# Graph convolution on one core: segment sums in one PSUM bank, edge attributes turned on chip, and VectorE's column picks moved to the end of each run

## The chip, the cores and the metric

The kernel runs on one core of a Trainium2 chip. The metric is the device time of one execution in microseconds (us): 3691.56 us is the median of 10 runs of the kernel before (3687.99 to 3696.28). Engines are named as in the profile: PE is TensorE (matrix products), DVE is VectorE, ACT is ScalarE, POOL is GpSimd, SP is SyncE. SP and POOL do no arithmetic here worth speaking of; they issue DMAs.

## The reference, cut to what matters

12,500 nodes carry 128 numbers each (32 scalars and 32 vectors of 3). 412,500 edges are sorted by target node; each has a source node, 4 attributes and 8 radial numbers.

```
f        = x @ W1            (128 -> features used by edges, and a part kept by the node)
e        = f[src]            gather by source node, 412,500 rows of 128 numbers
w        = gelu(gelu(ea8 @ Wm1) @ Wm2) @ Wp      128 weights per edge
message  = products of w, e and the 4 attributes ea4
n        = segment_sum(message, dst)
y        = keep * f_self + mix * (n @ W2)
out      = layernorm(x + y)
```

## The kernel before

The edges are cut into 806 **runs** of 512 (4 quarters of 128 edges, one edge per partition), and 4 runs make a **chunk**, so there are 202 chunks. One loop (`for s in range(NCH * CH + CH)`) goes over the runs; `s` is the run, `c, k = divmod(s, 4)` its chunk and its place in it. The order in which each of PE, ACT, DVE and SP issues its work is the order of the calls in this loop: the schedule is written by hand, and each engine works its list strictly in that order. POOL has a list too, but only of gathers.

A first stage of some 150 us loads `x`, writes `x @ W1` as `table` to memory and keeps `x` transposed in `xT`. Then, for each run `s`:

- **Gathering the rows of `f`.** `gather(s + 19)` (line 194) issues up to four indirect DMAs on POOL, one per quarter, 19 runs ahead into a ring of 20 tiles `G`. Three other ways take quarters off POOL: every 14th run one quarter is fetched row by row by SP (`aid`, L184); and `COLS = {DVE: 5, ACT: 7}` says that DVE takes one quarter in 5 runs and ACT one in 7. They **pick** 128 columns of `xT`, one at a time, by a node number that stands in a register: `pick_nodes` (L154) loads the registers of this run's share from on-chip memory (a `TENSOR_LOAD`), `pick` copies (L165 on DVE, L167 on ACT). `picked_rows` (L173, L174) multiplies the finished quarter by `W1`.
- **Weights.** `radial` (L458, L460), `mlp1` (L467, L471), `mlp2` (L482, L487) for a chunk, `weights` (L499) for two runs, on PE and ACT.
- **Messages.** `messages(s)` (L538, L541) is three products on DVE: weights from PSUM times gathered rows, into `M` of 128 x 4 quarters x 2 halves x 128.
- **Selection.** `select(c + 1)` (L525, L529), at k = 3, makes for each edge a row `S` of 4 attributes x 8 places: the attribute where the edge's target is the j-th of its quarter's 8 nodes, zero elsewhere.
- **Segment sums.** `segments(s - 1)` (L550) multiplies `S` by `M` on PE: 4 products with 32 columns of weights and 256 columns of data into a PSUM tile of 128 x 256 with a single buffer; ACT copies it to `SG` (L553). Of its 256 columns, only the first 128 are used for attribute 0 and only the last 128 for attributes 1 to 3.
- **Placing.** `placing(s)` (L559) makes on DVE a 128 x 128 matrix of zeros and ones; `place(c - 1)` (L566, L567), at k = 1, multiplies with it, two products a run, so that sums stand in a window of 32 nodes. `add(c - 1)` (L572, L577), at k = 2, loads four window positions into registers and adds the four windows into the sums `A` on DVE, one after the other.
- **Norm.** 24 times, when the chunk's nodes are complete, `norm` (L594 to L625) finishes 512 nodes. Four clears of the next sums (L365) follow, one a run.

The list of VectorE for one run is therefore: messages (3 products), placing, register load, picks (24 or 28 copies), and then, by k, the additions (k = 2) or the norm and the selection (k = 3) or a clear. The list of SP holds, besides the aid rows, two loads per chunk, of `ea8` (128 x 16 x 8) and `ea4` (128 x 16 x 4; L449), the latter in pieces of 16 bytes.

Of the kernel before, what the change touches and what calls it, by code (L numbers as in the profile page):

```python
# [44 lines left out]
STEPS = 12  # L45
COLS = {DVE: 5, ACT: 7}
COL_Q = {DVE: Q - 2, ACT: Q - 3}
# [5 lines left out]
def gnn_kernel(ctx: ExitStack, tc: tile.TileContext, x, src, dst, ea4, ea8, w1_0, w1_1, wm1, wm2,  # L53
# [54 lines left out]
    for e, per in COLS.items():  # L108
        picked[e], (t, k) = [], COL_TURN[e]
        while True:  # L110
            at = t + per + 1
            at += (k - at) % CH
            if at + 2 >= NS - 1:
                break
            picked[e].append((t, at, at + 2))
            t += per
    pick_of = {(e, s): i for e, g in picked.items() for i, (_, _, s) in enumerate(g)}
# [7 lines left out]
    def aid_load():  # L125


        nc.sync.dma_start(aid_at, sub(src, AID_FROM * SB + (Q - 1) * P, [[AID * SB, len(aided)], [1, P]]))
        nc.vector.tensor_scalar(aid_at, aid_at, float(4 * P), None, op0=OP.mult)
        for e, g in picked.items():  # L130
            cycle = CH // math.gcd(CH, COLS[e])
            for h in range(0, len(g), P):
                part = g[h:h + P]
                rows = cst.tile([len(part), P], I32, name=f"pick{len(pick_rows)}")
                for i in range(min(cycle, len(part))):
                    n = len(part[i::cycle])
                    nc.sync.dma_start(rows[i::cycle], sub(src, part[i][2] * SB + COL_Q[e] * P,
                                                          [[cycle * COLS[e] * SB, n], [1, P]]))
# [6 lines left out]
    def pick_nodes(e, s):  # L145

        per = COLS[e]
        i, t = divmod(s - COL_TURN[e][0], per)
        if not 0 <= i < len(picked[e]):
            return  # L150
        if t == 0:
            GT[e, i] = wk.tile([P, P], F32, name=f"gt{list(picked).index(e)}", bufs=3)
        r0, r1 = (n * (P // 4) // per * 4 for n in (t, t + 1))
        _, r = nc.values_load_multi_w_load_instructions(  # L154
            pick_rows[e, i][:, r0:r1], engines=[e], min_val=x_at, max_val=x_at + 4 * (N - 1),
            skip_runtime_bounds_check_because="addresses of columns")
# [137 lines left out]
    def clear():  # L294
        nc.vector.memset(wpost, 0.0)
        nc.vector.memset(ones, 1.0)
        nc.vector.memset(odd, 0.0)

    def weight_loads():
# [89 lines left out]

    raws = {}  # L390

    def load_raws(b):
        raws[b] = [load_run_rows(dst, b, NO_NODE), load_run_rows(src, b, 0)]

    def load_indices(b):
# [4 lines left out]
        for kind, raw in zip((1, 0), raws.pop(b)):  # L400
            f = wk.tile([P, SB], F32, name="rawf")
            nc.vector.tensor_copy(f[:ns, :], raw[:ns, :])
            if kind:
                g = wk.tile([P, SB], F32, name="rawr", bufs=1)
                off = against_window(f, g, ns)
# [14 lines left out]

    def load_run_rows(a, b, fill):
        ns = min(P, NS - b * P)
        part = b * P + ns == NS and REM < SB
        fl = ns - 1 if part else ns
        raw = wk.tile([P, SB], I32, name="raw")
# [8 lines left out]
    e4, e8, eT, H1, H2, WP, S, M, PL, SG, ST = {}, {}, {}, {}, {}, {}, {}, {}, {}, {}, {}  # L434

    def load_edges(b):
        s0 = b * CH
        ns = min(CH, NS - s0)
        e4[b] = wk.tile([P, CH, Q, 4], F32, name="e4", bufs=EDGES_AHEAD)
# [3 lines left out]
        if part:  # L443
            nc.vector.memset(e4[b][:, fl], 0.0)
        if fl < CH:
            nc.vector.memset(e8[b][:, fl:], 0.0)
        for a, t, n in ((ea8, e8[b], RAD), (ea4, e4[b], 4)):
            if fl:
                nc.sync.dma_start(t[:, :fl].rearrange("p s q k -> p (s q) k"),  # L449
                                  sub(a, s0 * SB * n, [[n, P], [P * n, fl * Q], [1, n]]))  # L450
            if part and RQ:
                nc.sync.dma_start(t[:, fl, :RQ, :], sub(a, (s0 + fl) * SB * n, [[n, P], [P * n, RQ], [1, n]]))
            if part and RP:
                nc.sync.dma_start(t[:RP, fl, RQ, :], sub(a, ((s0 + fl) * SB + RQ * P) * n, [[n, RP], [1, n]]))

# [64 lines left out]
    def select(c):  # L520

        n = min(CH, NS - c * CH)
        b, r = divmod(c * CH, P)
# [3 lines left out]
                                .to_broadcast([P, n, Q, J]), op=OP.is_equal)  # L527
        S[c] = wk.tile([P, CH * Q, 4, J], F32, name="S")
        nc.vector.tensor_tensor(S[c][:, :n * Q],  # L529
                                oh[:, :n].rearrange("p s q j -> p (s q) j")[:, :, None, :]  # L530
                                .to_broadcast([P, n * Q, 4, J]),
                                e4[c][:, :n].rearrange("p s q k -> p (s q) k")[:, :, :, None]
                                .to_broadcast([P, n * Q, 4, J]), op=OP.mult)

# [10 lines left out]
    def segments(s):  # L545

        c, r = divmod(s, CH)
        pt = ps.tile([P, 2 * P], F32, name="seg", bufs=1)
        for q in range(Q):
            nc.tensor.matmul(pt[q * W:(q + 1) * W, :], S[c][:, r * Q + q].rearrange("p k j -> p (k j)"),  # L550
                             M[s][:, q].rearrange("p a u -> p (a u)"), start=True, stop=True)
        SG[s] = wk.tile([P, 2 * P], F32, name="sg", bufs=CH + 2)
        nc.scalar.activation(SG[s], pt, AF.Copy)  # L553

    def placing(s):

        b, r = divmod(s, P)
        PL[s] = wk.tile([P, P], F32, name="pl", bufs=CH + 1)
        nc.vector.tensor_scalar(PL[s], iota, colv[b][:, r:r + 1], None, op0=OP.is_equal)  # L559

    def place(c):
        ns = min(CH, NS - c * CH)
        ST[c] = pt = ps.tile([P, CH, 4, W], F32, name="m", bufs=1)
        for k in range(ns):
            s = c * CH + k
            nc.tensor.matmul(pt[:, k, 0, :], SG[s][:, :P], PL[s][:, :W], start=True, stop=True)  # L566
            nc.tensor.matmul(pt[:, k, 1:, :].rearrange("p a n -> p (a n)"), SG[s][:, P:], PL[s][:, W:],  # L567
                             start=True, stop=True)

# [187 lines left out]
    with tc.manual_schedule(engines={PE, ACT, DVE, SP}):  # L757
# [7 lines left out]
        for b in range(min(3, NG)):  # L765
# [3 lines left out]
        loads = list(weight_loads())  # L769
        extra = {2: lambda: load_edges(0), 4: lambda: load_raws(0), NG // 2: lambda: load_indices(0),  # L770
                 NG // 2 + 3: make_w1b, NG // 2 + 5: make_ws, NG - 6: lambda: radial(0), NG - 4: lambda: mlp1(0),
# [36 lines left out]
        for s in range(NCH * CH + CH):  # L808
# [7 lines left out]
            if s % P == P // 2 and (s // P + 1) * P < NS:  # L816
                load_indices(s // P + 1)
            for t in range(P // ROWS):
                a = s + AID_LEAD - t * STEPS // (P // ROWS)
                if a in aided:  # L820
                    aid(a, t)
# [9 lines left out]
            if k == (0 if end else 1) and 0 < c <= NCH:  # L831
                place(c - 1)
            for e in picked:
                if (e, s + 2) in pick_of:
# [57 lines left out]
```

## Time and profile before

| what | value |
|---|---|
| median of 10 runs | 3691.56 us (3687.99 to 3696.28) |
| the profiled execution, its own time | 3696.46 us |
| its span, first to last instruction | 3694.7 us |
| busy: PE, DVE, ACT, POOL | 2878.0, 3061.6, 2277.2, 2764.9 us |
| granted TensorE clock, mean | 0.783 |
| DMA moved, mean | 244.14 MB, 66 GB/s |

A page of the profile gives groups of instructions by line: engine, operation, tiles written and read, count; then busy us and mean ns of one; then the idle time of the engine ahead of them and what ended it. "issue" is idle time that ended without anything that the profile can name, for example while the engine's own sequencer was busy with instructions that are not counted as work (register loads, semaphore operations). Names with q (DVEq) are such instructions of a sequencer. The profile's span is 1.8 us below the execution's own time, and that is 4.9 us above the median of the runs.

### The profile page before, as it was taken

The page shows a single profiled execution, that of the slowest core. Times are in us where ns is not written, and L with a number is a line of the kernel's source. Part 1 is how long each engine was busy: PE and PEld are TensorE (multiplying, and loading weights), DVE is VectorE, ACT ScalarE, POOL GpSimd, SP SyncE. Part 2 cuts the span into 40 slices and gives each one's busy share as a digit, 9 for nine tenths or more (in the row PEclk, how much of TensorE's full clock was granted, in tenths as well). Part 3 has the DMA queues.
Part 4 walks back from the last instruction along what each step waited for, and adds up shares of the span by engine and source line. Part 5 has one row for each costly group of instructions (what it writes and reads, how often), then busy time and mean ns, then how long its engine had stood idle before and what let it go on. Part 6 is the DMA issues. An engine that isn't in the chain of part 4 may idle for free. (4 is left out here: it accounts for less than half of the span.)

```text
span 3694.7 us, 117877 instructions
## 1 busy us (share of the span) xinstructions
PE 2878.0 (78%) x24857; PEld 2046.5 (55%) x24857; DVE 3061.6 (83%) x25248; ACT 2277.2 (62%) x16665; POOL 2764.9 (75%) x2906
## 2 busy tenths in 40 slices
PE   5788788777788877778778788878787888777787
PEld 5555565455456555555555455555555655555555
DVE  3699898889898888887888888878888888788885
ACT  2366666666576666565666566666566666566564
POOL 6777777777777777777777777777777777777775
PEclk7878777888777788786787777777777777787776
DMA  8223333333333333333333333333333333333331
GB/s 200 55 56 66 66 62 61 61 68 66 60 66 62 62 66 66 61 66 61 62 67 66 60 66 61 62 65 67 62 60 66 61 62 65 63 61 65 62 61 47
DMA packets 990429, 244.14 MB, mean 66 GB/s; under 512 B 896838, under 2 KB 941705, under 8 KB 989699
## 3 DMA queue, kind: packets, MB, share of 16 engines
q0 software_dynamic: 92768, 190.17, 17.7%
q1 hardware_dynamic: 876673, 39.90, 14.4%
q10 hardware_dynamic: 20258, 6.46, 0.7%
q14 instruction: 532, 4.36, 0.4%
q8 instruction: 198, 3.24, 0.3%
HBM read 223.49 MB, written 12.80 MB: 64 GB/s over the span
## 5 line engine op out<-in xcount | busy, mean ns | idle before, releaser
L194 POOL DMA_INDIRECT G<-table,idx x2835 | 2703.4, 954 | 882.6 <-issue 680.2
L165 DVE COPY gt<-xT 128x1 f32 x20224 | 1302.0, 144 | 248.4 <-issue 237.9
L167 ACT ACTIVATE gt<-xT 128x1 f32 x14336 | 1448.7, 192 | 37.4 <-issue 34.3
L550 PE MATMUL seg<-M,S 128*32 128x256 f32 x6448 | 630.7, 469 | 486.7 <-DVE M L541 383.6
L499 PE MATMUL w<-wpb,h 64*128 64x128 f32 x6448 | 716.1, 356 | 108.5 <-DVE M L541 107.6
L541 DVE TENSOR_TENSOR M<-w,G 128x384 f32<-128x384 f32 x1580 | 799.4, 548 | 0.0
L553 ACT ACTIVATE sg<-seg 128x256 f32<-128x256 f32 x806 | 305.6, 379 | 747.9 <-PE seg L550 693.7
L499 PEld LDWEIGHTS w<-wpb,h 64*128 64x128 f32 x6448 | 595.3, 249 | 243.3 <-DVE M L541 132.9
L567 PE MATMUL m<-pl,sg 128*128 128x96 f32 x1612 | 505.2, 410 | 0.0
L550 PEld LDWEIGHTS seg<-M,S 128*32 128x32 f32 x6448 | 145.2, 119 | 621.0 <-issue 210.1
L538 DVE TENSOR_TENSOR M<-w,G 128x256 f32<-128x256 f32 x790 | 324.1, 410 | 135.1 <-DMA G<-table,idx 88.1
L566 PEld LDWEIGHTS m<-pl,sg 128*128 128x128 f32 x1612 | 357.9, 274 | 119.3 <-issue 113.5
L566 PE MATMUL m<-pl,sg 128*128 128x32 f32 x1612 | 383.1, 327 | 5.1 <-ACT sg L553 3.4
L567 PEld LDWEIGHTS m<-pl,sg 128*128 128x128 f32 x1612 | 372.1, 284 | 0.0
L467 PEld LDWEIGHTS h<-eT,w1b 64*128 64x128 f32 x3232 | 274.3, 254 | 148.6 <-issue 139.2
L482 PE MATMUL h<-h,w2b 64*64 64x256 f32 x3232 | 313.1, 399 | 50.8 <-ACT h L471 47.9
L467 PE MATMUL h<-eT,w1b 64*128 64x128 f32 x3232 | 318.2, 354 | 8.8 <-ACT eT L460 8.8
L174 ACT ACTIVATE G<-h 128x128 f32<-128x128 f32 x270 | 74.1, 275 | 342.1 <-PE h L173 303.4
L482 PEld LDWEIGHTS h<-h,w2b 64*64 64x64 f32 x3232 | 139.4, 134 | 231.1 <-ACT h L471 190.8
L577 DVE TENSOR_TENSOR acc<-m,acc 128x128 f32 x806 | 234.2, 291 | 33.2 <-issue 3.5
L471 ACT ACTIVATE h<-h 128x512 f32<-128x512 f32 x404 | 217.8, 591 | 64.5 <-PE h L467 60.1
L559 DVE TENSOR_SCALAR pl<-iota,colv 128x128 f32<-128x128 f32 x806 | 237.0, 294 | 8.3 <-PE m L567 8.2
(109 smaller groups left out, 1709.2 us busy)
## 6 DMA issues: line engine op xcount, KB each, us to landing
G<-table SPq DMA_DIRECT2D x7040, 0.5 KB
G<-table,idx POOLq DMA_INDIRECT x2835
e<-in_edge_attr SPq DMA_DIRECT2D x201, 64.0 KB
e<-in_edge_attr SPq DMA_DIRECT2D x201, 32.0 KB
xt<-in_x SPq DMA_DIRECT2D x24, 256.0 KB
table<-ft ACTq DMA_DIRECT2D x24, 256.0 KB
out<-y SPq DMA_DIRECT2D x24, 256.0 KB
raw<-in_dst SPq DMA_DIRECT2D x6, 256.0 KB
```

The source lines that it names most:

```text
L165: nc.vector.tensor_copy(to, col)
L167: nc.scalar.activation(to, col, AF.Copy)
L194: nc.gpsimd.indirect_dma_start(out=G[s][:, q, :], out_offset=None, in_=x if s < raw_runs else table, in_offset=bass.IndirectOffsetOnAxis(a ...
L467: nc.tensor.matmul(p1[h][:, j // 2, j % 2, :], w1b[rows, j, :], eT[c][rows, :], start=True, stop=True)
L482: nc.tensor.matmul(p2[r][k * HID:(k + 1) * HID, h * n:(h + 1) * n], w2b[rows, :], H1[c][h][rows, k * n:(k + 1) * n], start=True, stop=True)
L499: nc.tensor.matmul(WP[i][:, q, :], H2[c][q % 2][rows, k, q // 2, :], wpb[rows, :], start=True, stop=True)
L538: nc.vector.tensor_tensor(m[:, :, :, :MUL], w[:, :, :2 * MUL].rearrange("p q (a u) -> p q a u", a=2), g[:, :, None, :MUL].to_broadcast([P, ...
L541: nc.vector.tensor_tensor(m[:, :, j, MUL:].rearrange("p q (i u) -> p q i u", i=3), w[:, :, None, (2 + j) * MUL:(3 + j) * MUL].to_broadcast ...
L550: nc.tensor.matmul(pt[q * W:(q + 1) * W, :], S[c][:, r * Q + q].rearrange("p k j -> p (k j)"), M[s][:, q].rearrange("p a u -> p (a u)"), s ...
L553: nc.scalar.activation(SG[s], pt, AF.Copy)
L566: nc.tensor.matmul(pt[:, k, 0, :], SG[s][:, :P], PL[s][:, :W], start=True, stop=True)
L567: nc.tensor.matmul(pt[:, k, 1:, :].rearrange("p a n -> p (a n)"), SG[s][:, P:], PL[s][:, W:], start=True, stop=True)
```

## The change

Five things are changed.

1. **Sums of both halves in one place.** `S` becomes two buffers `S_own` that are cleared once; per edge they hold 56 columns: 8 for attribute 0, then 24 that stay zero, then 24 for attributes 1 to 3. `segments` multiplies twice per quarter, columns 0 to 31 with the first half of `M` and columns 24 to 55 with the second half, and lets PSUM add them. One 128 x 128 result a run is left, four runs share a PSUM bank, ACT copies two runs at a time, and `place` needs one product a run. `select` writes the attribute-0 part and the rest in two products.
2. **Attributes turned on chip.** `ea4` is loaded for 32 runs at once, 128 rows of 2 KB (`load_attributes`), and four PE transposes and one ACT copy bring it into place (`turn_attributes`).
3. **Placing matrices by chunk.** `placing(c)` makes four of them in one instruction, at k = 0.
4. **Order of VectorE's list.** `pick_nodes` and `pick` stand at the end of a run, behind the additions, the norm, the clear (now only at k = 1) and the selection.
5. **More picks.** `COLS = {DVE: 4.5, ACT: 6}`: DVE takes 2 quarters in 9 runs (175 in all instead of 158, in shares of 32, 24 or 28 copies), ACT one in 6 (130 instead of 112). POOL has 2800 gathers from `table` left instead of 2835.

Buffers for index rows are shared with others (`rows_tile`). The diff, cut to its core:

```diff
-COLS = {DVE: 5, ACT: 7}
+COLS = {DVE: 4.5, ACT: 6}
...
     def pick_nodes(e, s):
-        per = COLS[e]
-        i, t = divmod(s - COL_TURN[e][0], per)
-        if not 0 <= i < len(picked[e]):
+        if (e, s) not in step_of:
             return
+        i, t = step_of[e, s]
+        per = len(picked[e][i][0])
...
+    S_own = [cst.tile([P, CH * Q, 2 * W - J], F32, name=f"S{i}") for i in range(2)]
...
+    def load_attributes(b):
+        full, rest = divmod(min(E - b * P * P, P * P), P)
+        t = e4_raw[b] = rows_tile(None if b else 2)
...
+        if full:
+            nc.sync.dma_start(t[:full], sub(ea4, b * P * P * 4, [[4 * P, full], [1, 4 * P]]))
...
+    def turn_attributes(b):
+        pt = ps.tile([P, 4, P], F32, name="h")
+        raw = e4_raw.pop(b).rearrange("t (e k) -> t k e", k=4)
+        for k in range(4):
+            nc.tensor.transpose(pt[:, k, :], raw[:, k, :], ident)
+        e4[b] = wk.tile([P, 4, P], F32, name="e4")
+        nc.scalar.activation(e4[b], pt, AF.Copy)
...
     def select(c):
...
-        nc.vector.tensor_tensor(S[c][:, :n * Q],
-                                oh[:, :n].rearrange("p s q j -> p (s q) j")[:, :, None, :]
-                                .to_broadcast([P, n * Q, 4, J]),
-                                e4[c][:, :n].rearrange("p s q k -> p (s q) k")[:, :, :, None]
-                                .to_broadcast([P, n * Q, 4, J]), op=OP.mult)
+        own = S_own[c % 2][:, :n * Q]
+        nc.vector.tensor_tensor(own[:, :, :J], hot, a[:, :, 0:1].to_broadcast([P, n * Q, J]), op=OP.mult)
+        nc.vector.tensor_tensor(own[:, :, W:].rearrange("p t (k j) -> p t k j", j=J),
+                                hot[:, :, None, :].to_broadcast([P, n * Q, 3, J]),
+                                a[:, :, 1:, None].to_broadcast([P, n * Q, 3, J]), op=OP.mult)
...
     def segments(s):
-        pt = ps.tile([P, 2 * P], F32, name="seg", bufs=1)
-        for q in range(Q):
-            nc.tensor.matmul(pt[q * W:(q + 1) * W, :], S[c][:, r * Q + q].rearrange("p k j -> p (k j)"),
-                             M[s][:, q].rearrange("p a u -> p (a u)"), start=True, stop=True)
...
-        nc.scalar.activation(SG[s], pt, AF.Copy)
+        if r == 0:
+            SEG[c] = ps.tile([P, CH, P], F32, name="seg", bufs=1)
+            SG[c] = wk.tile([P, CH, P], F32, name="sg")
+        own = S_own[c % 2]
+        for h, col in enumerate((0, W - J)):
+            for q in range(Q):
+                nc.tensor.matmul(SEG[c][q * W:(q + 1) * W, r, :], own[:, r * Q + q, col:col + W], M[s][:, q, h, :],
+                                 start=h == 0, stop=h == 1)
+        if r % 2 or s == NS - 1:
+            nc.scalar.activation(SG[c][:, r // 2 * 2:r + 1, :], SEG[c][:, r // 2 * 2:r + 1, :], AF.Copy)
...
-    def placing(s):
-        nc.vector.tensor_scalar(PL[s], iota, colv[b][:, r:r + 1], None, op0=OP.is_equal)
+    def placing(c):
+        nc.vector.tensor_tensor(PL[c][:, :n], iota[:, None, :].to_broadcast([P, n, P]),
+                                colv[b][:, r:r + n, None].to_broadcast([P, n, P]), op=OP.is_equal)
...
     def place(c):
-            nc.tensor.matmul(pt[:, k, 0, :], SG[s][:, :P], PL[s][:, :W], start=True, stop=True)
-            nc.tensor.matmul(pt[:, k, 1:, :].rearrange("p a n -> p (a n)"), SG[s][:, P:], PL[s][:, W:],
-                             start=True, stop=True)
+            nc.tensor.matmul(pt[:, k].rearrange("p a n -> p (a n)"), SG[c][:, k, :], PL[c][:, k, :], start=True, stop=True)
...
+            if s % ET == 8 and s - 8 + ET < NS:
+                load_attributes(s // ET + 1)
...
+            if s % ET == 21 and s - 21 + ET < NS:
+                turn_attributes(s // ET + 1)
...
             if s < NS:
                 messages(s)
-                placing(s)
-                pick_nodes(DVE, s)
-                pick(DVE, P)
+                if k == 0:
+                    placing(c)
...
             if k == (1 if end else 2) and 0 < c <= NCH:
                 add(c - 1)
             if k == (1 if end else 3) and 0 < c <= NCH:
                 norm(due.get(c - 1, []), last=c == NCH)
...
-            elif clearing:
+            elif k == 1 and clearing:
                 clear_sums(clearing.pop(0)[1])
             if k == 3 and c + 1 < NCH:
                 select(c + 1)
+            if s < NS:
+                pick_nodes(DVE, s)
+                pick(DVE, P)
```

More of the change, by code (lines that the diff above doesn't have):

```diff
@@ L108, in gnn_kernel @@
     for e, per in COLS.items():
-        picked[e], (t, k) = [], COL_TURN[e]
+        picked[e], (t0, k) = [], COL_TURN[e]
         while True:
-            at = t + per + 1
+            t, z = (t0 + int(n * per) for n in (len(picked[e]), len(picked[e]) + 1))
+            at = z + 1
             at += (k - at) % CH
@@ L114, in gnn_kernel @@
                 break
-            picked[e].append((t, at, at + 2))
-            t += per
+            picked[e].append((range(t, z), at, at + 2))
+    step_of = {(e, s): (i, s - g[i][0][0]) for e, g in picked.items() for i in range(len(g)) for s in g[i][0]}
     pick_of = {(e, s): i for e, g in picked.items() for i, (_, _, s) in enumerate(g)}
@@ L130, in aid_load @@
         for e, g in picked.items():
-            cycle = CH // math.gcd(CH, COLS[e])
+            cycle = next(n for n in range(1, P) if n * COLS[e] % CH == 0)
             for h in range(0, len(g), P):
@@ L137, in aid_load @@
                     nc.sync.dma_start(rows[i::cycle], sub(src, part[i][2] * SB + COL_Q[e] * P,
-                                                          [[cycle * COLS[e] * SB, n], [1, P]]))
+                                                          [[int(cycle * COLS[e]) * SB, n], [1, P]]))
                 nc.vector.tensor_scalar(rows, rows, 4.0, float(x_at), op0=OP.mult, op1=OP.add)
@@ L297, in clear @@
         nc.vector.memset(odd, 0.0)
+        for t in S_own:
+            nc.vector.memset(t, 0.0)
     def weight_loads():
@@ L390, in gnn_kernel, with rows_tile @@
     raws = {}
+    scratch = wk.tile([P, 4, ACC], F32, name="acc")
+    def rows_tile(part=None):
+        if part is None:
+            return wk.tile([P, XB, P], F32, name="xt", bufs=3).rearrange("p q e -> p (q e)")
+        return scratch[:, part, :SB]
     def load_raws(b):
-        raws[b] = [load_run_rows(dst, b, NO_NODE), load_run_rows(src, b, 0)]
+        raws[b] = [load_run_rows(dst, b, NO_NODE, None if b else 0), load_run_rows(src, b, 0, None if b else 1)]
     def load_indices(b):
@@ L400, in load_indices @@
         for kind, raw in zip((1, 0), raws.pop(b)):
-            f = wk.tile([P, SB], F32, name="rawf")
+            f = wk.tile([P, XB, P], F32, name="ft", bufs=3).rearrange("p q e -> p (q e)")
             nc.vector.tensor_copy(f[:ns, :], raw[:ns, :])
             if kind:
-                g = wk.tile([P, SB], F32, name="rawr", bufs=1)
+                g = wk.tile([P, XB, P], F32, name="ft", bufs=3).rearrange("p q e -> p (q e)")
                 off = against_window(f, g, ns)
@@ L419, in load_indices, with load_run_rows @@
             nc.vector.tensor_copy((rel if kind else idx)[b][:, :, :ns], pt[:, :, :ns])
-    def load_run_rows(a, b, fill):
+    def load_run_rows(a, b, fill, part_of):
         ns = min(P, NS - b * P)
@@ L424, in load_run_rows @@
         fl = ns - 1 if part else ns
-        raw = wk.tile([P, SB], I32, name="raw")
+        raw = rows_tile(part_of).bitcast(I32)
         if part:
@@ L431, in load_run_rows @@
         return raw
-    e4, e8, eT, H1, H2, WP, S, M, PL, SG, ST = {}, {}, {}, {}, {}, {}, {}, {}, {}, {}, {}
+    e4, e8, eT, H1, H2, WP, M, PL, SEG, SG, ST = {}, {}, {}, {}, {}, {}, {}, {}, {}, {}, {}
+    S_own = [cst.tile([P, CH * Q, 2 * W - J], F32, name=f"S{i}") for i in range(2)]
     def load_edges(b):
@@ L438, in load_edges @@
         ns = min(CH, NS - s0)
-        e4[b] = wk.tile([P, CH, Q, 4], F32, name="e4", bufs=EDGES_AHEAD)
         e8[b] = wk.tile([P, CH, Q, RAD], F32, name="e8", bufs=EDGES_AHEAD)
@@ L442, in load_edges @@
         fl = ns - 1 if part else ns
-        if part:
-            nc.vector.memset(e4[b][:, fl], 0.0)
+        t = e8[b]
         if fl < CH:
[L446 to L454, printed above, removed]
+            nc.vector.memset(t[:, fl:], 0.0)
+        if fl:
+            nc.sync.dma_start(t[:, :fl].rearrange("p s q k -> p (s q) k"),
+                              sub(ea8, s0 * SB * RAD, [[RAD, P], [P * RAD, fl * Q], [1, RAD]]))
+        if part and RQ:
+            nc.sync.dma_start(t[:, fl, :RQ, :], sub(ea8, (s0 + fl) * SB * RAD, [[RAD, P], [P * RAD, RQ], [1, RAD]]))
+        if part and RP:
+            nc.sync.dma_start(t[:RP, fl, RQ, :], sub(ea8, ((s0 + fl) * SB + RQ * P) * RAD, [[RAD, RP], [1, RAD]]))
+    ET = P // Q
+    e4_raw = {}
+    def load_attributes(b):
+        full, rest = divmod(min(E - b * P * P, P * P), P)
+        t = e4_raw[b] = rows_tile(None if b else 2)
+        if full < P:
+            nc.vector.memset(t, 0.0)
+        if full:
+            nc.sync.dma_start(t[:full], sub(ea4, b * P * P * 4, [[4 * P, full], [1, 4 * P]]))
+        if rest:
+            nc.sync.dma_start(t[full:full + 1, :4 * rest], sub(ea4, (b * P + full) * P * 4, [[4 * rest, 1], [1, 4 * rest]]))
+    def turn_attributes(b):
[5 more added lines that the diff above has]
+        nc.scalar.activation(e4[b], pt, AF.Copy)
     def radial(c):
@@ L527, in select @@
                                 .to_broadcast([P, n, Q, J]), op=OP.is_equal)
-        S[c] = wk.tile([P, CH * Q, 4, J], F32, name="S")
-        nc.vector.tensor_tensor(S[c][:, :n * Q],
-                                oh[:, :n].rearrange("p s q j -> p (s q) j")[:, :, None, :]
-                                .to_broadcast([P, n * Q, 4, J]),
-                                e4[c][:, :n].rearrange("p s q k -> p (s q) k")[:, :, :, None]
-                                .to_broadcast([P, n * Q, 4, J]), op=OP.mult)
+        hot = oh[:, :n].rearrange("p s q j -> p (s q) j")
+        t0 = c * CH % ET * Q
+        a = e4[c * CH // ET][:, :, t0:t0 + n * Q].rearrange("p k t -> p t k")
+        own = S_own[c % 2][:, :n * Q]
[3 more added lines that the diff above has]
+                                a[:, :, 1:, None].to_broadcast([P, n * Q, 3, J]), op=OP.mult)
     def messages(s):
@@ L547, in segments @@
         c, r = divmod(s, CH)
-        pt = ps.tile([P, 2 * P], F32, name="seg", bufs=1)
-        for q in range(Q):
-            nc.tensor.matmul(pt[q * W:(q + 1) * W, :], S[c][:, r * Q + q].rearrange("p k j -> p (k j)"),
-                             M[s][:, q].rearrange("p a u -> p (a u)"), start=True, stop=True)
-        SG[s] = wk.tile([P, 2 * P], F32, name="sg", bufs=CH + 2)
-        nc.scalar.activation(SG[s], pt, AF.Copy)
-    def placing(s):
-        b, r = divmod(s, P)
-        PL[s] = wk.tile([P, P], F32, name="pl", bufs=CH + 1)
-        nc.vector.tensor_scalar(PL[s], iota, colv[b][:, r:r + 1], None, op0=OP.is_equal)
+        if r == 0:
[9 more added lines that the diff above has]
+    def placing(c):
+        n = min(CH, NS - c * CH)
+        b, r = divmod(c * CH, P)
+        PL[c] = wk.tile([P, CH, P], F32, name="pl")
+        nc.vector.tensor_tensor(PL[c][:, :n], iota[:, None, :].to_broadcast([P, n, P]),
+                                colv[b][:, r:r + n, None].to_broadcast([P, n, P]), op=OP.is_equal)
     def place(c):
@@ L769, in gnn_kernel @@
         loads = list(weight_loads())
-        extra = {2: lambda: load_edges(0), 4: lambda: load_raws(0), NG // 2: lambda: load_indices(0),
+        extra = {2: lambda: load_edges(0), 3: lambda: load_attributes(0), NG // 2 - 2: lambda: turn_attributes(0), 4: lambda: load_raws(0), NG // 2: lambda: load_indices(0),
                  NG // 2 + 3: make_w1b, NG // 2 + 5: make_ws, NG - 6: lambda: radial(0), NG - 4: lambda: mlp1(0),
```

## The prediction

> **What bounds the kernel now.** I read the page first (busy time, groups), then the waits of POOL and of DVE, then the register loads by their line, then single runs in the timeline.
>
> Groups of the page; behind the bar busy us, mean ns, idle time before and what ended it:
>
> ```profile
> L194 POOL DMA_INDIRECT G<-table,idx x2835 | 2703.4, 954 | 882.6 <-issue 680.2
> L165 DVE COPY gt<-xT 128x1 f32 x20224 | 1302.0, 144 | 248.4 <-issue 237.9
> ```
>
> Waits of POOL and of DVE (us in total, times, longest):
>
> ```profile
> POOL G L194 <- issue: 699.7, 2293, 0.6
> POOL G L194 <- DMA G<-table,idx: 109.8, 360, 0.3
> POOL G L194 <- DVE M L541: 23.1, 59, 5.4
> ```
>
> ```profile
> DVE gt L165 <- issue: 237.9, 481, 2.8
> DVE M L538 <- DMA G<-table,idx: 88.1, 70, 4.6
> ```
>
> POOL never stands still for another engine: the 0.30 us ahead of each gather is a fixed gap, so gathers follow each other without a break from 200 us to 3669 us, 1593 of them in the 2000 us from 1500 to 3500 us: one per 1.255 us. POOL sets the pace. But VectorE is only just faster. It waits for gathered rows 88.1 us, and 19.0 us for SP's rows, in all the span: 3%. The rest of its 16% idle time is mostly the 237.9 us ahead of the picks. Their cause is in the register loads of L154 (min/median/max ns):
>
> ```profile
> L154 DVEq TENSOR_LOAD <-pick x790: 1598/1694/2993, 153.4 to 3635.8; - x198
> ```
>
> Timeline, VectorE's lines of 1800 to 1818 us (start, us, instruction, idle time before):
>
> ```profile
> 1801.25 0.41 DVE L538 TENSOR_TENSOR M<-w,G 128x256 f32<-128x256 f32 x1
> ...
> 1801.58 1.01 DVE L541 TENSOR_TENSOR M<-w,G 128x384 f32<-128x384 f32 x2
> ...
> 1802.51 0.28 DVE L559 TENSOR_SCALAR pl<-iota,colv 128x128 f32<-128x128 f32 x1
> ...
> 1803.17 1.79 DVE L165 COPY gt<-xT 128x1 f32 x28 [0.39 <-issue]
> ...
> 1805.04 1.27 DVE L577 TENSOR_TENSOR acc<-m,acc 128x128 f32 x4
> ```
>
> Here the load for 28 registers ran from 1801.20 to 1803.08, and the first pick began 0.09 us later. So it is nearly everywhere: of 778 runs between 200 and 3630 us, 91% begin their picks within 0.15 us of the load's end. **The load, not the placing, decides when the picks start**: 1.84 us (mean) behind the start of the messages, which with the placing are done after 1.56 us.
>
> When may the load start? It stands in the sequencer's list behind instructions that wait. The register operations (L577, 69 ns) between the four additions tell: each addition waits for the one before, and in the 193 groups of this stretch the operation behind the second addition starts 14 ns (median; 90% within 15) after that addition has started, never ahead of it. Behind the selection's product, which waits for its one-hot, the sequencer's next event again comes 14 ns (median) after its start. **Nothing passes a waiting instruction.** The additions stand behind the picks today, so no load waits for them.
>
> **The change, part by part.** A chunk is four runs, and I count VectorE per chunk. Before, runs 20 to 800 start at 209.3 and 3648.5 us: 17.64 us a chunk. It closes: 4 x 1.84 to the first picks; 25.6 picks a run at 61.4 ns, 6.29; additions 1.31; one-hot and selection 0.93; clears 0.26; norms about 0.6 and index turns 0.3 spread over all chunks; waits for rows 0.5; in all 17.6.
>
> *Loads and what now stands ahead of them.* A load takes 1.67 us (mean) for 24 registers and 1.93 for 28, so 0.066 a register; the 0.35 us (median) of L572's four lie on that line. No row shows 32: on the line 2.20, if it were flat 1.93. I take 2.20, since three sizes lie on it. With 352 loads of 32, 261 of 24 and 174 of 28, the mean is 1.96 instead of 1.78. From the start of the messages to the first pick:
> - k = 0: messages 1.27, then the placing of 128 x 512, bounded by L559 (0.29) and L529 (0.69, of which the next instruction sees 0.61). I take 0.61, the same size: 1.88. A load with picks ahead of it starts 0.2 us before the messages and is ready at 2.10 with 32 registers, so 1.98 on average.
> - k = 1: no placing; by the load 1.87, with a clear ahead of it in half of the chunks 1.91: 1.89.
> - k = 2: the first addition starts at 1.27, the fourth at 2.25 (three starts 0.327 apart), the load then: 2.26 + 1.96 + 0.10 = 4.33.
> - k = 3: one-hot at 1.27, first selection product at 1.58, load at 1.63: 3.69. The second product runs beneath the load, whatever it costs.
>
> Sum 11.89 instead of 7.37: **+4.52**. This is a new stall of about 1.7 us behind the additions and 1.3 us behind the selection. Queued behind it are the picks, then the next messages, and PE's segment products wait for those.
>
> *More picks.* 2176 x 61.4 ns = 134 us over 197 chunks: +0.68.
>
> *Gone from behind the picks*: additions 1.31 and selection 0.93, whose time now lies in the figures above, and clears 0.26: -2.50.
>
> *Given back.* With VectorE late, its waits for rows go (97.5 us between 200 and 3640 us, 0.50 a chunk), those for PE (24 us, 0.12), and about half of the 50.7 us ahead of the norm's statistics (0.12), because additions precede them by more: -0.74.
>
> Net 4.52 + 0.68 - 2.50 - 0.74 = **+1.96 us** a chunk, 197 chunks: +386 us. At the end five waits for the last rows (9.6 us between 3643 and 3661 us) go. At the start, eight more pick loads on SP (0.70 us each) stand against earlier attribute loads: +2, and 2 x 0.85 us of clears on an idle VectorE: nothing. Sum 3696.5 + 386 - 10 + 2 = 4074 on the profiled execution; the median lies 4.9 below, and I round down to **4065**.
>
> *The other engines.* POOL loses 35 gathers, 35 x 1.255 = 43.9 us, all hidden if VectorE is late. PE: a place goes from four instructions a run to two (0.85 us to about 0.43), the segments from 8 instructions with 256 columns (0.64 us) to 16 with 128: between 0.64 (same columns) and 1.28 (every instruction as long); -0.42 to +0.22 us a run beside 4.9. ACT: 2304 picks at 101 ns add 233, 35 rows 10, 26 attribute turns of 0.60 us 16, and 403 evictions of 0.38 us fall away, 153: 2277 + 106 = 2383 us of 4065, 59% busy. SP drops 201 loads of 16-byte pieces, and its 105.3 us of waits for the selection with them; the aid rows queued behind come sooner, worth at most the 19.0 us above, already counted. None of these is on the path while VectorE is.
>
> [...]
>
> **Rivals.**
> 1. *POOL stays the bound.* The load passes the waiting additions and products: k = 2 then takes 2.58, k = 3 2.20, the four 8.65, net 1.28 + 0.68 - 2.50 - 0.74 = -1.28, or 16.4 us a chunk, under POOL's 14.16 gathers x 1.255 = 17.8. Then the 35 gathers count: 3696.5 - 43.9 = 3652.6, **3648** on the median. It decides if the two stalls come out over 1.9 us a chunk smaller than I have them. For it: DVE is 83% busy by the page, and its idle "issue" looks free. Against it: the 193 groups.
> 2. *The additions hold the load only until the first of them has its sums from PE*: 0.98 us a chunk less, 193 us: **3872**. Against it: the operations between the additions would then bunch, and they do not.
> 3. *The change does not bring its picks forward at all, because PE or ACT becomes late*: PE's bound of +0.22 us a run over 806 runs is 177 us on 2878 busy, 75% of 4065, so this needs stalls that nothing shows.
>
> **How the numbers follow.** Forecast 0.80: 4065; its own range takes the flat load of 32 registers (0.44 us a chunk, 87 us), a placing of 0.29 (18 us) down, to 3960, and the two smallest gifts not given (47 us) and a load 0.1 us longer a chunk (20 us) up, to 4135. Rival 1: 0.13. Rival 2: 0.06. Rival 3 and the rest: 0.01. The range reaches down to rival 2 and leaves out rival 1: 3870 to 4135. About 0.2% is what a measurement here can tell from no change; faster 0.13, same 0.01, slower 0.86.
>
> **What would show it.** In the profile after: idle time ahead of the picks (issue) goes from 237.9 us to some 700, with the longest behind the additions and the selection; the loads start at the fourth addition's start and at the first selection product's; POOL's waits for VectorE's messages (a full ring) go from 23.1 us to hundreds; VectorE no longer waits for rows; the load for 32 registers reads 2.2 us. If POOL still runs without gaps and the waits for gathered rows stay, I am wrong, and the sequencer does pass waiting instructions.

## The result, and the profile after

The changed kernel takes **4048.47 us** (median of 8 runs, 4046.37 to 4055.36) against 3691.12 us for the kernel before (median of 28): 1.097 times as long, 95% interval 1.0961 to 1.098. The profiled execution took 4052.88 us, its span 4051.1 us. The forecast was 4065 us.

The engines on the page of the kernel after (busy us, share of the span, instructions):

```profile
PE 2845.4 (70%) x29867; PEld 2112.8 (52%) x29867; DVE 3148.3 (78%) x27022; ACT 2409.7 (59%) x18627; POOL 2751.3 (68%) x2871
```

No engine is busier than before by more than 133 us (ACT, through the picks it gained), and every engine's share has fallen. So nobody got 356 us of work; somebody waits. The groups of the same page:

```profile
L195 POOL DMA_INDIRECT G<-table,idx x2800 | 2689.7, 961 | 1186.9 <-issue 771.6
L166 DVE COPY gt<-xT 128x1 f32 x22400 | 1430.5, 144 | 665.1 <-issue 655.0
L571 DVE TENSOR_TENSOR M<-w,G 128x256 f32<-128x256 f32 x790 | 327.2, 414 | 0.6 <-ACT G L175 0.2
```

The idle time ahead of the picks rose from 237.9 us to 655.0. The first product of the messages, the instruction that uses the gathered rows, waited 0.6 us in all: VectorE is now always later than the rows. POOL's own waits say the same from the other side (us in total, times, longest):

```profile
POOL G L195 <- issue: 790.2, 2505, 3.7
POOL G L195 <- DVE M L574: 311.8, 159, 12.2
...
POOL G L195 <- DMA G<-table,idx: 8.5, 28, 0.3
```

Waits of POOL for VectorE's messages, which free a buffer of the ring, were 23.1 us and are 311.8. They come seldom and are long (up to 12.2 us), as fits a ring that POOL can fill before it has to wait.

And VectorE's waits:

```profile
DVE gt L166 <- issue: 655.0, 513, 2.5
DVE bst L644 <- ACT y L640: 69.3, 23, 6.0
```

The register loads, first all of VectorE's in the kernel after (min/median/max ns), then, by narrower windows, the two that answer to the timeline below:

```profile
L155 DVEq TENSOR_LOAD <-pick x787: 1598/1948/2539, 149.5 to 3994.6; - x197
...
L155 DVEq TENSOR_LOAD <-pick x1: 2389/2389/2389, 2004.8 to 2004.8; - x1
...
L155 DVEq TENSOR_LOAD <-pick x1: 2194/2194/2194, 2010.9 to 2010.9; - x1
```

VectorE in the timeline of the kernel after, the runs k = 2 and k = 3 of one chunk (start, us, instruction, idle time before). L556 is the one-hot, which marks for each edge which of its quarter's 8 nodes is its target; the two products of the selection (L563, L564) use it:

```profile
2002.59 0.42 DVE L571 TENSOR_TENSOR M<-w,G 128x256 f32<-128x256 f32 x1
2002.92 1.02 DVE L574 TENSOR_TENSOR M<-w,G 128x384 f32<-128x384 f32 x2
2003.85 1.27 DVE L615 TENSOR_TENSOR acc<-m,acc 128x128 f32 x4
2007.32 2.03 DVE L166 COPY gt<-xT 128x1 f32 x32 [2.20 <-issue]
2009.26 0.41 DVE L571 TENSOR_TENSOR M<-w,G 128x256 f32<-128x256 f32 x1
2009.59 1.01 DVE L574 TENSOR_TENSOR M<-w,G 128x384 f32<-128x384 f32 x2
2010.52 0.28 DVE L556 TENSOR_TENSOR oh<-iota,rel 128x128 f32<-128x128 f32 x1
2010.84 0.29 DVE L563 TENSOR_TENSOR S<-oh,e 128x128 f32<-128x128 f32 x1
2011.05 0.55 DVE L564 TENSOR_TENSOR S<-oh,e 128x384 f32<-128x384 f32 x1
2013.13 2.21 DVE L166 COPY gt<-xT 128x1 f32 x32 [1.53 <-issue]
```

Read it with the loads. The fourth addition starts at 2004.82 and the load 14 ns later; it lasts 2.39 us; the first pick comes at 2007.32, 2.20 us after the additions are done. One run later the first selection product starts at 2010.84, the load 16 ns later for 2.19 us, the first pick at 2013.13. VectorE has nothing to do in between but the second product. In runs 20 to 800, the 194 loads behind four additions start 14 ns (median; 10th to 90th percentile 13 to 15) after the fourth addition's start, and the 193 loads behind a selection 16 ns (15 to 17) after its first product's start.

### The profile page after: what moved, and what is told of

It is laid out like the page before. It is cut to its first block, busy times and chain, and to the rows that moved or that the text cites. A ratio compares the mean times of both kernels' runs of the same rounds, so it can differ in the third digit from the quotient of the medians.

```text
span 4051.1 us, 131101 instructions
## 1 busy us (share of the span) xinstructions
PE 2845.4 (70%) x29867; PEld 2112.8 (52%) x29867; DVE 3148.3 (78%) x27022; ACT 2409.7 (59%) x18627; POOL 2751.3 (68%) x2871
## 5 line engine op out<-in xcount | busy, mean ns | idle before, releaser
L166 DVE COPY gt<-xT 128x1 f32 x22400 | 1430.5, 144 | 665.1 <-issue 655.0
L168 ACT ACTIVATE gt<-xT 128x1 f32 x16640 | 1663.8, 191 | 148.9 <-issue 147.6
L588 PE MATMUL seg<-M,S 128*32 128x128 f32 x12896 | 694.8, 344 | 509.2 <-DVE M L574 388.9
L588 PEld LDWEIGHTS seg<-M,S 128*32 128x32 f32 x12896 | 366.5, 130 | 708.6 <-issue 284.8
L591 ACT ACTIVATE sg<-seg 128x256 f32<-128x256 f32 x403 | 151.7, 377 | 702.7 <-PE seg L588 689.6
L606 PE MATMUL m<-pl,sg 128*128 128x128 f32 x1612 | 379.4, 409 | 6.9 <-ACT sg L591 5.2
L606 PEld LDWEIGHTS m<-pl,sg 128*128 128x128 f32 x1612 | 323.6, 298 | 75.6 <-issue 67.8
L501 ACT ACTIVATE h<-h 128x512 f32<-128x512 f32 x404 | 216.3, 586 | 37.6 <-PE h L497 36.7
L517 ACT ACTIVATE h<-h 128x512 f32<-128x512 f32 x404 | 214.4, 581 | 15.2 <-PE h L512 9.5
L174 PE MATMUL h<-wf,gt 128*128 128x128 f32 x610 | 171.7, 379 | 0.0
L174 PEld LDWEIGHTS h<-wf,gt 128*128 128x128 f32 x610 | 157.8, 314 | 0.0
```

The lines of the kernel that those rows point to most:

```text
L166: nc.vector.tensor_copy(to, col)
L168: nc.scalar.activation(to, col, AF.Copy)
L174: nc.tensor.matmul(pt, GT.pop((e, i)), wf, start=True, stop=True)
L588: nc.tensor.matmul(SEG[c][q * W:(q + 1) * W, r, :], own[:, r * Q + q, col:col + W], M[s][:, q, h, :], start=h == 0, stop=h == 1)
L606: nc.tensor.matmul(pt[:, k].rearrange("p a n -> p (a n)"), SG[c][:, k, :], PL[c][:, k, :], start=True, stop=True)
```

## The experiments

The theory: a waiting VectorE instruction holds its sequencer, so the load for the picks cannot start before the last waiting instruction ahead of it has started, and VectorE stands idle for what is left of the load. The first rival: the loss comes from something else in the change (longer loads, the new placing or selection, segments in one bank, the share of the picks), and the order is innocent. All kernels change the kernel after, except where it says otherwise. The kernel before is run beside them on the same chip.

**Order undone.** The load and the picks go back behind the messages and the placing; the rest of the change stays.

```diff
                 if k == 0:
                     placing(c)
+                pick_nodes(DVE, s)
+                pick(DVE, P)
...
-            if s < NS:
-                pick_nodes(DVE, s)
-                pick(DVE, P)
```

> All of the change but the order: VectorE's register load and picks stand behind the placing again, ahead of additions, norm, clear and selection. If the register load held behind waiting additions and products is the cause, the stalls of 1.83 us (k = 2) and 1.28 us (k = 3) a chunk shrink to the 0.2 to 0.5 us of the kernel before; the longer loads (0.18 us a run) and the 11% more picks (0.68 us a chunk) remain, so VectorE needs about 18.4 us a chunk against 17.64 before: 3800 to 3860 us. If the extra picks or the new segment sums are the cause, it stays near 4048 us.

Measured: 3683.42 us against 3699.28, ratio 0.9958 (0.9944 to 0.9973). VectorE's waits, first line:

```profile
DVE gt L166 <- issue: 292.8, 471, 1.6
```

The loss is gone whole, and more: the rest of the change is worth -16 us, where I had expected it to cost 100 to 160. I had charged the longer loads in full. They are longer by 0.18 us, but they also start sooner, at k = 1 above all: 0.33 us ahead of the messages' start (median) instead of 0.13 us behind it. So the first picks of a chunk come 7.37 us behind the messages, summed over its four runs, as before. That the two sums agree to the hundredth is chance. Why the loads start sooner was not tried, but the trace of the kernel before has an answer that fits the theory: there the placing at k = 1 waits for PE's place products, which use its buffer, and in 123 of 195 runs the load starts within 60 ns (mostly 50 to 52) after such a product has ended. The change has no placing at k = 1.

**Order alone.** The kernel *before*, with nothing changed but the place of the picks.

```diff
                 messages(s)
                 placing(s)
-                pick_nodes(DVE, s)
-                pick(DVE, P)
...
                 select(c + 1)
+            if s < NS:
+                pick_nodes(DVE, s)
+                pick(DVE, P)
```

> The kernel before with the order alone changed: register load and picks last in each run, everything else as before. Held load: k = 2 begins its picks some 4.4 us and k = 3 some 3.7 us behind the messages, 4.0 us a chunk more, less 2.5 us of additions, selection and clears that no longer follow, less 0.6 us of waits given back: about +1 us a chunk, 3870 to 3920 us. If the extra picks or the new sums are the cause: 3691 us, no change.

Measured: 3970.42 us, 1.0732 (1.0713 to 1.0752): slower by 271 us, 50 more than the upper end. Its waits of VectorE, and below them the norm's line in the kernel before:

```profile
DVE gt L165 <- issue: 650.2, 611, 2.3
DVE bst L606 <- ACT y L602: 93.6, 24, 5.4
...
DVE bst L606 <- ACT y L602: 55.3, 24, 4.6
```

The stall ahead of the picks is as large as in the kernel after (237.9 us before, 650.2 here, 655.0 there), without any other part of the change. A part of the miss is in the second line: the waits ahead of the norm's statistics rose from 55.3 to 93.6 us, where I had counted on a gift. With these two runs the first rival falls: the order alone makes 271 of the 357 us, and without it there is no loss. The other 86 us come only where the order and the rest of the change (longer loads, more picks) meet; no run splits them.

**Load ahead, picks last.** Only the load moves forward; the order of VectorE's own instructions is exactly that of the kernel after.

```diff
                     placing(c)
+                pick_nodes(DVE, s)
...
             if s < NS:
-                pick_nodes(DVE, s)
                 pick(DVE, P)
```

> The changed kernel with one thing moved: the register load stands directly behind messages and placing, ahead of additions, norm and selection; the order of the engine's own instructions is exactly that of the changed kernel, picks last. Held load: the load no longer waits for additions or products, but they now wait for it; about 0.7 us less at k = 2 and 0.7 us less at k = 3, 1.4 us a chunk, 280 us: about 3770 us (3740 to 3800). If the order of the engine's work is the cause (messages late for PE, whatever the load does): 4048 us, no change.

Measured: 3752.41 us, 1.0138 (1.0118 to 1.0158). Of the 357 us above the kernel before, 53 are left, by moving one instruction of VectorE's sequencer. What is left shows in VectorE's waits:

```profile
DVE acc L615 <- PE seg L588: 97.1, 96, 1.5
...
DVE oh L556 <- issue: 71.1, 137, 1.2
DVE acc L615 <- issue: 52.5, 55, 1.6
DVE gt L166 <- issue: 47.3, 104, 1.1
```

The picks hardly wait now, but whatever stands behind the load waits for it instead: the one-hot 71.1 us, the additions 52.5. The first line belongs here too, though the profile names PE: in runs 20 to 800, the place products that the additions read had ended 6.0 us (median) before the first addition started, and in 191 of 195 chunks the load for the picks, the load of the four window positions and a register operation follow each other without a pause of more than 0.1 us, and the addition starts some 53 ns behind them. The idle time ahead of the first addition is 195.7 us in all, 1.0 us a chunk. A load holds the instructions behind it as a waiting instruction holds the load.

**No loads.** VectorE's picks copy fixed columns, so the register loads go; this leaves out VectorE's part of the gather by node number. The order stays that of the kernel after.

```diff
+        if e == DVE:
+            for k in range(r1 - r0):
+                picking[e].append((GT[e, i][:, r0 + k:r0 + k + 1], xT[:, r0 + k:r0 + k + 1]))
+            return
```

> The changed kernel without VectorE's register loads: its picks copy the fixed columns 0 to 127 of the turned nodes, so the part of the gather by node number that VectorE does is left out. Held load: the 655 us of idle time ahead of the picks go, VectorE needs some 16.2 us a chunk, and POOL sets the pace with 35 gathers less than before: 3648 us (3635 to 3665). If the copies and the new order themselves are too much for VectorE: above 3800 us.

Measured: 3656.88 us, 0.9887 (0.9869 to 0.9905). VectorE's waits, first line:

```profile
DVE M L575 <- DMA G<-table,idx: 212.2, 194, 3.8
```

With the loads away, VectorE waits for gathered rows again and POOL sets the pace: 42 us under the kernel before, near the 43.9 us of the 35 gathers that POOL has lost. So without the loads the order costs nothing that reaches the time. What it may cost VectorE otherwise does not show here, since POOL sets the pace.

**Wait gone.** The one-hot for the next chunk is made at k = 1 instead of k = 3. At k = 3 the same two selection products stand ahead of the load, but no longer wait for the one-hot just ahead of them.

```diff
                     placing(c)
+                if k == 1 and c + 1 < NCH:
+                    one_hot(c + 1)
...
-        oh = wk.tile([P, CH, Q, J], F32, name="oh", bufs=1)
+        oh = OH[c] = wk.tile([P, CH, Q, J], F32, name="oh", bufs=1)
```

It ran first on another chip, together with three more kernels: the kernel after with the old share of picks (`COLS = {DVE: 5, ACT: 7}`), the order undone with that share, and a version with the loads covered, described below.

> The changed kernel with one wait gone: the one-hot for the next chunk is made at k = 1 instead of k = 3, so the selection's products still stand ahead of the load and the picks at k = 3, but wait for nothing. Held load: the load then starts with the messages and runs beneath both products; the picks at k = 3 begin 2.0 us behind the messages instead of 3.8: 1.65 us a chunk less, about 3720 us (3690 to 3770). If what stands ahead of the load delays it whether it waits or not: 4040 us.

> The changed kernel, its order too, with the picks of the kernel before (VectorE 1 quarter in 5 runs, ACT 1 in 7). Held load: the two stalls stay, only their loads are 0.18 us shorter and 0.68 us of copies a chunk are less: about 1.1 us a chunk, so 3820 to 3850 us, far above the 3691 us before. If the extra picks are the cause: 3691 us.

> The kernel before with the new segment sums, the turned attributes and the placing by chunk alone: old order, old shares of picks. POOL has as many gathers as before and VectorE and PE have no more to do than before: 3691 us (3680 to 3700), no change. If the new sums cost something of their own: above 3720 us.

> A version meant to beat both: shares of picks and sums of the changed kernel; ahead of each run's load stands only work that waits for nothing of VectorE (placing and one-hot at k = 3, clear at k = 1), and additions, norm and the selection's products stand behind the picks. Held load: VectorE needs about 17.0 us a chunk, less than POOL's 17.8, so POOL sets the pace with 35 gathers less: about 3650 us (3640 to 3665), 1.2% faster than before.

On that chip everything took some 5450 us, the kernel before too (5464.59); I call it a late chip. VectorE in the timeline of the order undone with the old share:

```profile
2023.50 0.21 DVE L166 COPY gt<-xT 128x1 f32 x2 [0.58 <-issue]
2024.25 0.15 DVE L166 COPY gt<-xT 128x1 f32 x1 [0.53 <-issue]
2024.95 0.15 DVE L166 COPY gt<-xT 128x1 f32 x1 [0.54 <-issue]
2025.66 0.15 DVE L166 COPY gt<-xT 128x1 f32 x1 [0.56 <-issue]
```

Picks that follow each other every 61 ns elsewhere come here one per 0.7 us for microseconds, and the profile names nothing that they wait for. The times are therefore **inconclusive** for this question: 5442.04 us for the wait gone (0.9957, 0.9933 to 0.9982), 5441.51 for the old share (0.9961, 0.9941 to 0.998), 5482.24 for the order undone with the old share (1.0026, 1.0006 to 1.0046), 5433.71 for the covered version (0.9929, 0.9902 to 0.9956). Only the idle time just ahead of the first pick can still be read. With the old share of picks in the new order it is 1.65 us a run at k = 2 and 1.07 at k = 3, so the stalls don't come from the new share; with the wait gone it is 1.82 and 0.18.

The same kernel on a third chip, where the kernel before takes 3693.0 us:

> The same kernel as in e7_wait_gone (the one-hot made two runs earlier, so that the selection's products wait for nothing), again, since there every kernel ran at some 5450 us. Held load: 3720 us (3690 to 3770) where the kernel before takes 3691. If what stands ahead of the load delays it whether it waits or not: 4040 us.

Measured: 3761.56 us, 1.0179 (1.0162 to 1.0196). VectorE in its timeline, k = 2 and k = 3:

```profile
2004.75 1.25 DVE L620 TENSOR_TENSOR acc<-m,acc 128x128 f32 x4
2007.69 1.54 DVE L166 COPY gt<-xT 128x1 f32 x24 [1.69 <-issue]
...
2010.42 0.27 DVE L568 TENSOR_TENSOR S<-oh,e 128x128 f32<-128x128 f32 x1
2010.62 0.54 DVE L569 TENSOR_TENSOR S<-oh,e 128x384 f32<-128x384 f32 x1
2011.09 1.77 DVE L166 COPY gt<-xT 128x1 f32 x28
```

Behind the additions, which wait for each other, the stall is there as in the kernel after. Behind the selection products, which now wait for nothing, the picks follow without a break. In the mean the idle time at k = 2 is 1.82 us (1.83 in the kernel after) and at k = 3 0.16 (1.28). The loads tell the same: at k = 3 they start 0.28 us (median) ahead of the messages, past both products, where in the kernel after they start 1.59 us behind the messages' start. This is the sharpest of the runs: the same two products stand ahead of the load at k = 3, and only the one-hot (0.28 us) and the wait for it have gone from there. It is the wait that holds the load.

The table puts runs on ordinary chips side by side. A chunk is the mean over runs 20 to 800, idle is the mean just ahead of the first pick, by k.

| kernel | time / before there (us) | chunk (us) | idle k = 0, 1, 2, 3 (us) |
|---|---|---|---|
| before | 3691.12 | 17.64 | 0.15, 0.46, 0.17, 0.45 |
| after | 4048.47 / 3691.12 | 19.52 | 0.05, 0.20, 1.83, 1.28 |
| order undone | 3683.42 / 3699.28 | 17.63 | 0.04, 0.38, 0.26, 0.83 |
| order alone | 3970.42 / 3699.28 | 19.08 | 0.12, 0.43, 1.59, 1.17 |
| load ahead | 3752.41 / 3699.28 | 17.99 | 0.06, 0.19, 0.00, 0.00 |
| no loads | 3656.88 / 3699.28 | 17.45 | 0.00, 0.00, 0.00, 0.00 |
| wait gone | 3761.56 / 3693.00 | 18.03 | 0.05, 0.12, 1.82, 0.16 |

**Loads covered.** A version meant to beat both: the order undone, and VectorE's work that does not wait put ahead of the picks where there was none to hide a load, the rest behind them.

```diff
-                if k == 0:
+                if k == (0 if end else 3):
                     placing(c)
...
+            if k == 1 and clearing and not end and c < NCH:
+                clear_sums(clearing.pop(0)[1])
+            if k == 3 and c + 1 < NCH:
+                one_hot(c + 1)
+            if s < NS:
+                pick_nodes(DVE, s)
+                pick(DVE, P)
```

> The same kernel as in b1_covered, again for the same reason. Held load: VectorE has room, POOL sets the pace with 35 gathers less: about 3650 us (3640 to 3665) where the kernel before takes 3691, and below the 3683 us of e1_order_undone, where VectorE set the pace.

Measured: 3678.11 us against 3693.0, 0.9956 (0.9939 to 0.9973). That is short of what I expected, and beside its own kernel before it is no faster than the order undone (0.9958): the two intervals are nearly the same. VectorE is fast enough again, as its waits show:

```profile
DVE gt L166 <- issue: 217.6, 442, 1.3
DVE M L576 <- DMA G<-table,idx: 67.3, 59, 3.7
```

POOL runs without gaps but for some 0.31 us (mean) ahead of each gather, as in the kernel before (868.9 us in 2800 gathers, 882.6 in 2835). What eats most of the gain is in its group on the page of the covered version:

```profile
L195 POOL DMA_INDIRECT G<-table,idx x2800 | 2706.6, 967 | 868.9 <-issue 650.5 <-DMA G<-table,idx 116.2 <-DVE M L579 33.9
```

A gather takes 967 ns instead of 954. 2800 x 13 ns are 36 us of the 44 us that the 35 gathers should have brought. Which gathers take longer is in the last section. To get it back I made the placing by run again, as in the kernel before, and in a second kernel also moved picks from VectorE towards ACT (`COLS = {DVE: 4.5, ACT: 5}`):

```diff
-        nc.vector.tensor_tensor(PL[c][:, :n], iota[:, None, :].to_broadcast([P, n, P]),
-                                colv[b][:, r:r + n, None].to_broadcast([P, n, P]), op=OP.is_equal)
+        nc.vector.tensor_scalar(PL[c][:, k], iota, colv[b][:, r:r + 1], None, op0=OP.is_equal)
```

> As b1_covered, but the placing matrices are made run by run again, by a comparison with one tensor operand (128 x 128, L559 of the kernel before) instead of a product of two tensors by chunk. In the trace of b1_covered_again a gather on POOL takes 0.967 us in the mean, 0.954 before; those that overlap the placing by chunk take 1.029, those that overlap no product of two on-chip tensors 0.944. If such products slow the gathers, the gather falls to some 0.959 us, 2800 x 8 ns = 22 us: about 3656 us where the kernel before takes 3692 (3648 to 3668). If VectorE is the bound: 3678 us or more, as b1_covered_again, since it gets 0.2 us a chunk more to do.

> As b3_placing_by_run, with ACT picking 1 quarter in 5 runs instead of 1 in 6: 31 gathers less on POOL. If POOL is the bound: 31 x 1.26 = 39 us below b3_placing_by_run, about 3617 us (3605 to 3635). If ACT or VectorE sets the pace there: no faster than b3_placing_by_run.

Both met a late chip again (kernel before 5477.37 us): 5456.02 us, 0.9968 (0.9948 to 0.9987), and 5498.29 us, 1.0045 (1.0025 to 1.0064). Whether either beats the covered version on an ordinary chip stays open.

## Why the prediction was right, point by point

- **The mechanism held.** No load passes a waiting instruction in the kernel after: the loads start 14 ns (median of 194) behind the fourth addition's start, as the register operations between the additions had told, and the wait-gone run shows that it is the wait (the idle time at k = 3 falls from 1.28 to 0.16 us).
- **First picks.** Predicted 1.98, 1.89, 4.33 and 3.69 us behind the messages' start for k = 0 to 3. Measured means 1.95, 1.78 and 4.35, and for k = 3 a median of 3.78 (the mean, 4.26, holds the norms that now stand ahead too). The run k = 1 is 0.11 us shorter than I had it.
- **Loads.** Mean 1.95 us, predicted 1.96. The 352 loads of 32 registers take 2.17 us (mean), predicted 2.20; the two shown above, 2.19 and 2.39, are of this size. So it is the line, not the flat value.
- **Stalls.** Predicted 1.7 us at k = 2 and 1.3 at k = 3; measured 1.83 and 1.28. In the total, 655.0 us ahead of the picks, predicted some 700.
- **Given back.** The waits for rows went altogether. The half of the norm's wait did not: VectorE's wait for ACT there rose from 50.7 to 64.6 us between 200 us and the end, where I had it fall by half (-0.12 us a chunk; really +0.07). The additions do precede the norm's wait by more, as I had counted on (4.6 us instead of 3.5, mean). But the chain that the norm waits for, from the last addition by way of PE to the end of ACT's copy, takes 7.7 us instead of 5.5 (median), and I had left that at what it was. Why it grew was not tried. This is the one term with the wrong sign, 0.19 us a chunk.
- **The sum.** A chunk went from 17.64 to 19.52 us, +1.88, predicted +1.96. It closes: 195 chunks between runs 20 and 800 make +366.2 us, the start -2.0 (predicted +2), the end -7.7 (predicted -10), in all 356.4, the difference of the two spans (4051.1 - 3694.7). The forecast lies 16 us high because the chunk is 0.08 us shorter than its sum. The terms that I had too long, k = 1 (0.11) and the extra picks (VectorE's time in picks rose by 0.54 us a chunk, predicted 0.68), outweigh the gift that did not come (0.19). That the total comes within 0.4% is in part luck: errors of up to 0.19 us a chunk, 37 us in all, cancel. One reading was slightly off: between 1500 and 3500 us the trace has 1590 gathers, not 1593, one per 1.258 us; nothing rests on the difference.
- **The other engines.** ACT 2409.7 us busy, predicted 2383. PE's place, 888.3 us in two groups, became 379.4; its segments 630.7 became 694.8, between the two bounds. Neither sets the pace.
- **The rivals.** *POOL stays the bound* would have needed the loads to pass the waits; the no-loads run comes nearest to that, at 3656.88 us where this rival said 3648. *Held only until the first addition has its sums* is excluded by the 14 ns behind the fourth. *PE or ACT late* would have left the stalls ahead of the picks unexplained; with the order undone, the same PE and ACT work runs at 3683.42 us.

## What to carry to other kernels

In this kernel a register load behaves as an instruction of a second engine that takes its turn in the same list: it starts only when the last waiting instruction ahead of it has started (14 and 16 ns later in the kernel after), and holds everything behind it until it is done (in the load-ahead run this left VectorE idle for 71.1 us ahead of the one-hot). Look for the same elsewhere. Put it directly behind long instructions that wait for nothing, so that they run while it loads, and put chains of dependent instructions behind the work that needs the registers: with both, in the covered version, the idle time ahead of the picks is 217.6 us instead of 655.0. When a trace names nothing for the idle time, read the starts of the sequencer's own operations against the starts of the engine's instructions; here that told the loss to within 5% before anything was run.

## What the runs showed of the hardware that was not expected

**A gather takes longer while VectorE works on certain instructions with two tensors in SBUF.** Most gathers last 0.94 to 0.95 us (median 0.944 in the kernel before and in the kernel after). Those that overlap certain VectorE instructions last longer. Means between 300 and 3500 us, and the share over 1 us:

| VectorE instruction that the gather overlaps | kernel | mean us | over 1 us |
|---|---|---|---|
| additions (one input in PSUM) | before | 0.944 | 0% |
| placing, tensor against one column value | before | 0.946 | 1% |
| selection product, two tensors in SBUF | before | 1.042 | 38% |
| placing, tensor against tensor | after | 1.095 | 68% |
| placing, tensor against tensor | covered | 1.029 | 33% |
| selection products | covered | 1.10 | 29 to 39% |
| placing, without the one-hot behind it | covered | 0.945 | 0% |
| placing and one-hot both | covered | 1.084 | 54% |
| one-hot alone, tensor against tensor | covered | 0.956 | 9% |
| one-hot alone, tensor against tensor | before | 0.943 | 0% |
| none of placing, one-hot and selection | covered | 0.946 | 0% |

On the two late chips the placing by tensor against tensor (order undone, old share) shows 1.109 us and 84%, and the placing by run 0.947 us and 0%. The placing by tensor against tensor and the selection products read two tensors from SBUF, and most of their rows are long. But the short one-hot reads two as well and alone hardly lengthens a gather (0.943 and 0.956 us), and in the covered version neither does the placing where the gather does not reach the one-hot behind it (0.945 us); what decides is open. For this case it suggests that the one placing for four runs, a saving on VectorE (0.68 us for the four instead of 0.29 us for each), can lengthen the work of POOL, which sets the pace once VectorE does not. That these instructions are the cause rests on this comparison between instructions; a run on an ordinary chip that removes the placing by tensor against tensor alone is missing, and the late chips do not show the gain: the mean gather is 0.950 us there in the covered version and 0.951 with the placing by run.

**VectorE can be late without a wait to show for it.** With the order undone, POOL issues its last gather at 3627.3 us (3668.5 before) without a gap since 201 us, and VectorE waits 0.2 us for gathered rows; the span ends 50 us after the last gather instead of 26. So the ring of gathered rows can hide a VectorE that falls behind by little: the 41 us that POOL gained became 18 us of span.

**Two sets of experiments were slower throughout.** In two of the four, each on a chip of its own, the kernel before took 5465 and 5477 us, 48% longer. In the traces from these chips 1177 to 1549 of VectorE's picks start 0.4 to 1 us after the one before; in the kernels before and after on ordinary chips it is 0 and 1. Whether the chip or the occasion makes the difference was not tried.
